# Eight graph-attention aggregations as seven half-products each, with the differences, sums and scores that this needs

## The chip, the cores and the metric

The kernel runs on one core of a Trainium2 chip, as one program of 31606 instructions. The metric is the device time of one execution in microseconds (us), the median over several runs. A core has a matrix engine (TensorE, "PE" in the profile, with its weight loads as "PEld"), a vector engine (VectorE, "DVE"), a scalar engine (ScalarE, "ACT"), a general engine (GpSimd, "POOL"), and a queue for transfers (SyncE, "SP"). Each engine runs its own instructions in order and waits for the others by semaphores. Matmuls write to PSUM, a memory of eight banks; the other data live in SBUF. All is fp32 here, and an fp32 matmul shows as two records in the trace.

## The reference, cut to what matters

A network of four layers over 512 nodes with 768 features. Only the graph part of layer 0 changes, a graph attention (GAT) of eight heads followed by one of a single head:

```python
def gat_layer(x, W, a_s, a_d, b, edge_index, concat):
    n = x.shape[0]
    H, C = a_s.shape
    h = (x @ W).reshape(n, H, C)
    src, dst = (edge_index[0], edge_index[1])
    alpha_s = jnp.einsum('nhc,hc->nh', h, a_s)
    alpha_d = jnp.einsum('nhc,hc->nh', h, a_d)
    e = jax.nn.leaky_relu(alpha_s[src] + alpha_d[dst], NEG_SLOPE)
    m = jax.ops.segment_max(e, dst, num_segments=n)
    e = jnp.exp(e - m[dst])
    denom = jax.ops.segment_sum(e, dst, num_segments=n)
    alpha = e / (denom[dst] + EPS)
    msg = h[src] * alpha[:, :, None]
    out = jax.ops.segment_sum(msg, dst, num_segments=n)
    ...
h = gat_layer(x, W1, a_src1, a_dst1, b1, edge_list, concat=True)
h = jax.nn.elu(h)
out = gat_layer(h, W2, a_src2, a_dst2, b2, edge_list, concat=True)
```

W1 is 768 x 6144 (eight heads of 768), W2 is 6144 x 768. With 16384 edges over 512 nodes the kernel works on a dense 512 x 512 matrix: `cnt` holds how often each edge occurs, and the softmax over a node's edges becomes a row of weights, so that a head's aggregation is a plain product of weights and features.

## The kernel before

Token-major tensors are four tiles of 128 nodes; feature-major ones six tiles of 128 features. A block product is made by seven half-products in place of eight (Strassen's scheme in Winograd's form): `SplitA` makes four sums of the left operand's quarters (L410 to L413 chunk by chunk, L420 to L423 whole), `SplitB` three differences of the right one's and one in place (L438 to L441, always on POOL), and `strassen` runs the seven products chunk by chunk (matmuls at L512) and combines them with one ACT copy (L527) and five DVE additions that read PSUM (L551, L554, L555, L560, L564). `strassen_token` gives token-major results, `strassen_feature` feature-major ones, and `strassen_add` (L605) adds its results into a tensor that exists.

One head i of layer 0 goes through these steps.

- `heads(i)` multiplies the normed nodes by W1's block i with seven half-products (the copy of h out of PSUM is at L823) and then takes two scores per node from h, source and target (`node_scores`, L796: four DVE instructions over 128x768 each, which read h and a row of coefficients, both in SBUF).
- `edge_weights` turns the scores into weights (`weighing`): four transposes spread the source scores (`row_of`, L329), four max-reductions with a penalty for missing edges follow (L743, which reads PSUM and the bf16 tile `off`), then the target score is added on ACT (L753), a leaky relu on DVE (L754), exp on ACT (L755), counts and row sums on DVE (L756), and the division (L763). `off` is made once, at the end of `edge_counts`, by four ACT instructions.
- `turned` transposes the weights on PE (L787) and copies them to `edge_wT` (L205 on ACT, L207 on DVE).
- `aggregate` multiplies features and weights plainly: six feature tiles times four node tiles, 24 matmuls with 512 columns (L901), each feature tile followed by `elu` (L802 to L804 on ACT, L805 on DVE) into gT and, for every second tile, by gT's sums on POOL (L410 to L413).
- `project` multiplies gT by W2's block and adds the result into h2 with `strassen_add` (DVE additions at L918).

The order across heads is a pipeline. In pass i of the main loop, the transposes of head i−1 are interleaved with the products of head i (the list `background`, one step at each product, by `tick`; `delayed(n)` lets n products go first). Then comes the aggregation of head i−1, then the edge weights of head i, then the projection of head i−1. `pinned` keeps what it wraps behind the last instruction of each engine before it; other instructions may be reordered by a scheduler. The tile of weights (`edge_w`) has one buffer, the weight matrices two, and their differences (`tw`) two.

Before head 0, `edge_counts` builds `cnt` from one-hot products of the edges (a comparison per 128 edges on DVE or ACT, L705 among them; sums on POOL, L722 and L723); 40 of its steps run ahead of head 0, the others beside it. The weights of head 1 are loaded, and their differences taken on POOL, when pass 1 begins.

Of the kernel before, what the change touches and what calls it, by code (L numbers as in the profile page):

```python
# [18 lines left out]
P = 128  # L19
# [78 lines left out]
def kernel(ctx: ExitStack, tc: tile.TileContext, a: dict, out: bass.AP):  # L98
# [296 lines left out]
    class SplitA:  # L395


        def __init__(self, xT, eng, ready=True):
            h = KC // 2
            self.st = big_tile("sx")[:, : 4 * h * HT].rearrange("p (i k n) -> p i k n", i=4, k=h)  # L400
            self.eng = eng
            self.a11, self.a12 = xT[:, :h, :HT], xT[:, h:, :HT]
            self.a21, self.a22 = xT[:, :h, HT:], xT[:, h:, HT:]
            self.s = [None] + [self.st[:, i] for i in range(4)]
            if ready:
                self.all_sums()
# [18 lines left out]
    def ready(src):  # L425

        return SplitB(split_weights(src))

    class SplitB:


        def __init__(self, w):
            h = KC // 2
            tt = diff_tile("tw").rearrange("p (i k n) -> p i k n", i=3, k=h)
            b11, b12 = w[:, :h, :HC], w[:, :h, HC:]
            b21, b22 = w[:, h:, :HC], w[:, h:, HC:]
            for k in range(h):
                G.tensor_sub(tt[:, 0, k], b22[:, k], b12[:, k])  # L438
                G.tensor_sub(b12[:, k], b12[:, k], b11[:, k])  # L439
                G.tensor_sub(tt[:, 1, k], b22[:, k], b12[:, k])  # L440
                G.tensor_sub(tt[:, 2, k], b21[:, k], tt[:, 1, k])  # L441
            self.b11, self.b21, self.b22 = b11, b21, b22
            self.t = [None, b12, tt[:, 1], tt[:, 0], tt[:, 2]]

    background = []

# [51 lines left out]
    def strassen(A, B, use, feature, then=None, extra=None, fresh=False):  # L498
# [5 lines left out]

        def product(bank, a, b, c, start, stop):
            tick()
            for k in range(KC // 2):
                if feature:
                    l, r = b[:, k, ts(c, P)], a[:, k, :]
                else:  # L510
                    l, r = a[:, k, ts(c, P)], b[:, k, :]
                T.matmul(bank, l, r, start=start and k == 0, stop=stop and k == KC // 2 - 1,  # L512
                         skip_group_check=True)

        def done(c, i, j, bank):
# [143 lines left out]
    counts = tc.tile_pool(name="counts", bufs=1, side="right")  # L659
    gone = counts.__enter__()  # L660
    cnt = gone.tile([P, NT, N], FP, name="cnt")
    off = gone.tile([P, NT, N], BF, name="off")
    cnt_dram = tc.dram_tile([P, NT, N], FP, name="cnt_dram")

    def reloaded(pool):
# [4 lines left out]
    def edge_counts(gp):  # L670
# [24 lines left out]
        for g in range(n_groups):  # L695
            js = range(EC * g // n_groups, EC * (g + 1) // n_groups)
            acc = [psum() for _ in range(2)]
            for j in js:
                oh = hots[j % len(hots)]
                if (j % 2 if j < 40 else j % 3 == 2):  # L700
                    S.activation(oh[:, :N], nodes, AF.Abs, bias=neg[:, j : j + 1])
                    S.activation(oh[:, :N], oh[:, :N], AF.Relu, bias=1.0, scale=-1.0)
                else:
                    V.tensor_scalar(oh[:, :N], nodes, ef[:, 0, j : j + 1], None, op0=ALU.is_equal)
                V.tensor_scalar(oh[:, N:], near if j < 32 else nodes[:, :HT], ef[:, 1, j : j + 1], far[:, j : j + 1],  # L705
                                op0=ALU.is_equal, op1=ALU.mult)
                for u in range(2):
                    T.matmul(acc[u], oh[:, N + u * P : N + (u + 1) * P], oh[:, :N],
                             start=j == js[0], stop=j == js[-1])
                yield  # L710
            for u in range(2):
                low, high = cnt[:, u, :], cnt[:, 2 + u, :]
                t = gp.tile([P, N], FP, name="up_t", bufs=2)
                S.activation(t, acc[u], AF.Identity, bias=part, scale=1.0 / HI)
                if g == 0:
                    V.tensor_scalar(high, t, MAGIC, -MAGIC, op0=ALU.add, op1=ALU.add)
                    V.scalar_tensor_tensor(low, high, -HI, acc[u], op0=ALU.mult, op1=ALU.add)
                else:
                    V.tensor_scalar(t, t, MAGIC, -MAGIC, op0=ALU.add, op1=ALU.add)
                    r = gp.tile([P, N], FP, name="up_r", bufs=1)  # L720
                    V.scalar_tensor_tensor(r, t, -HI, acc[u], op0=ALU.mult, op1=ALU.add)
                    G.tensor_add(high, high, t)  # L722
                    G.tensor_add(low, low, r)  # L723
        for t in range(NT):
            S.activation(off[:, t, :], cnt[:, t, :], AF.Relu, bias=bigc, scale=-BIG)
        nc.sync.dma_start(cnt_dram, cnt)

    def several(steps, n):
# [5 lines left out]
            yield  # L734


    def weighing(w, src4, dst4, cnt, off):

        srow = row_of(src4)
        yield  # L740
        mx = tiny(NT, name="ga_mx")
        for t in range(NT):
            V.tensor_tensor_reduce(w[:, t, :], srow, off[:, t, :], 1.0, -3.0e38,  # L743
                                   ALU.subtract, ALU.max, mx[:, t : t + 1])
        V.tensor_add(mx, mx, dst4)
        nm = tiny(NT, name="ga_nm")
# [18 lines left out]
    def weight_tile(gp):  # L765
        return gp.tile([P, NT, N], FP, tag="edge_w", name="edge_w", bufs=1)

    def edge_weights(src4, dst4, gp, cnt, off):
        w = weight_tile(gp)
        for _ in weighing(w, src4, dst4, cnt, off):  # L770
            pass
        return w

# [30 lines left out]
        S.activation(dst, dst, AF.Exp, scale=-1.0)  # L804
        V.scalar_tensor_tensor(dst, dst, -1.0, ps, op0=ALU.add, op1=ALU.max)  # L805

    def last_gat(h, as_row, ad_row, gp, cnt, off, between=None):

        s4, d4 = node_scores(h, row(as_row), gp), node_scores(h, row(ad_row), gp)
        ew = edge_weights(s4, d4, gp, cnt, off)  # L810
        made = between() if between else None
        wT = by_source(ew, gp)
        token_product(by_chunk(wT), lambda s: h[:, s, :], add_to_x)
        return made


    open_products()

    def heads(i):
        w1 = split_weights(a["L0_gnn_W1"][:, i * D : (i + 1) * D])  # L820
        B = pinned(lambda: SplitB(w1)) if i == 1 else SplitB(w1)
        h = token_major("h")
        strassen_token(xs, B, lambda t, c, ps: S.copy(h[:, t, ts(c, HC)], ps), None,  # L823
                       None if i else n0.rest)
        flush()
        return h, node_scores(h, row(f"g0_as{i}"), gp), node_scores(h, row(f"g0_ad{i}"), gp)

    with tc.tile_pool(name="graph", bufs=1) as gp:
        counting = edge_counts(gp)
        for _ in range(24):  # L830
            next(counting)
        n0 = Norm(x, "xn", 1e-5)
        for t in (0, 2, 1, 3):
            n0.chunk(t)
            if t == 1:
                n0.first()
        xs = n0.split
        raw_xn = tc.dram_tile([P, NT, D], FP, name="raw_xn")
        nc.sync.dma_start(raw_xn, n0.n)
        for _ in range(16):  # L840
            next(counting)
        background.append(several(counting, 7))
        loose.append(background[0])
        head0 = heads(0)
        drain()

    qkv = a["L0_mix_qkv_w"]
# [44 lines left out]
    with tc.tile_pool(name="gat0", bufs=2) as gp:  # L892
        h2 = token_major("h2")

        def aggregate(i, h, wT, norm=None):
            gT = feature_major("gT")
            sums = SplitA(gT, G, False)
            for n, f in enumerate((0, 3, 1, 4, 2, 5)):
                ps = psum()
                for s in range(NT):  # L900
                    T.matmul(ps, h[:, s, ts(f, P)], wT[:, s, :], start=s == 0, stop=s == NT - 1)  # L901
                elu(gT[:, f, :], ps, col("g0_b1", i * KC + f))
                if norm and n < NT:
                    norm.chunk(n)
                if f >= KC // 2:
                    sums.sums(f - KC // 2)
            return sums

        def project(i, sums):
# [29 lines left out]
        for i in range(9):  # L939
            if done:  # L940
                g, hg, ew = done
                wT = gp.tile([P, NT, N], FP, tag="edge_wT", name="edge_wT", bufs=wt_bufs[0])
                if i < 8:
                    if i == 1:
                        background.append(delayed(5, weighing(ew, s4, d4, cnt, off)))
                    background.append(delayed(0 if i == 1 else 8, turned(ew, wT)))
                else:
                    for _ in turned(ew, wT):
                        pass
            if i < 8:  # L950
                h, s4, d4 = heads(i) if i else head0
                drain()
            if done:
                norm = performer_norm() if i == 8 else None
                sums = aggregate(g, hg, wT, norm)
            if i < 8:
                done = i, h, edge_weights(s4, d4, gp, cnt, off) if i else weight_tile(gp)
            else:
                ys, va = performer_values(norm)
            if i:  # L960
                project(g, sums)
            if i == 2:
                degrees()
        x = load_x()
        qT = last_gat(h2, "g0_as", "g0_ad", gp, cnt, off, lambda: performer_features(ys, 0))
        add_row_to(x, row("g0_b2"))
    counts.__exit__(None, None, None)

# [1084 lines left out]
```

## Time and profile before

| quantity | value |
|---|---|
| median of 3 runs | 3097.74 us (3096.92 to 3099.75) |
| profiled execution, its own time | 3099.04 us |
| its span in the trace | 3097.2 us |
| mean granted TensorE clock | 0.992 of full speed |
| first to last of five equal periods of a head (from 235.35 us to 628.97 us) | 78.73 us each |
| PE busy in such a period | 77.6 us |
| DVE, ACT, POOL busy in such a period | 39.2, 22.1, 34.7 us |

A row of the profile's groups reads: line, engine, operation, output and inputs, shape and count, then the busy time in us and the mean of one in ns, and then the time that the engine idled just before such instructions, with what ended it. In the chain of waits every piece is the instruction that the next one had to wait for. In lists of instructions the first number is the start and the second the length in us. A busy time of PE includes the modelled end of each matmul, which overlaps the next one, so that lengths of records add up to more than the time that passes; the distance between their starts does not.

### The profile page before, as it was taken

Reading aid. Unit: us, or ns where it says so; the run is one execution under the profiler, and the core shown is the slowest. Engines: PE = TensorE matmul, PEld = TensorE weight load, DVE = VectorE, ACT = ScalarE, POOL = GpSimd, SP = SyncE. Lnnn points to the kernel's source line nnn. Section 1 sums busy time; section 2 is a strip of 40 time slices with the busy share of each in tenths; the row PEclk is TensorE's granted clock in tenths of the full one; section 3 lists DMA queues with packets and bytes.
Section 4 is the critical chain, followed back from the end, with each engine's and each line's share of the span. In section 5 each row is a group of like instructions: output and inputs, shape, how many; then the busy total and the mean of one; then the engine's idle time right before and its main releaser. Section 6 shows DMA issues by size and latency. Waiting matters only on the chain.

```text
span 3097.2 us, 31606 instructions
## 1 busy us (share of the span) xinstructions
PE 3005.4 (97%) x11757; PEld 2006.2 (65%) x11757; DVE 1482.7 (48%) x3416; ACT 749.7 (24%) x1434; POOL 1436.3 (46%) x1532
## 2 busy tenths in 40 slices
PE   7899999999999999999899999999999999999989
PEld 3455555556766777765675367877777776677755
DVE  9854444556256235446766435333333335462341
ACT  7322222252252112004432213100000012221111
POOL 3544444442516663655651444455544557355610
PEclk9999999999999999999999999999999999999999
DMA  3112212223202222321111512122221223122222
GB/s 116 56 70 72 72 72 72 71 92 82 82 1 97 92 92 93 118 92 57 61 72 62 148 67 97 67 92 92 92 90 68 88 92 123 60 89 77 99 80 62
DMA packets 92691, 253.63 MB, mean 82 GB/s; under 512 B 9889, under 2 KB 14881, under 8 KB 91514
## 3 DMA queue, kind: packets, MB, share of 16 engines
q1 hardware_dynamic: 92538, 251.61, 23.5%
q8 instruction: 93, 1.52, 0.2%
q14 instruction: 60, 0.49, 0.1%
HBM read 244.23 MB, written 7.36 MB: 81 GB/s over the span
## 4 chain that ended last, share of the span: by engine, by line
PE 86%; DVE 8%; POOL 2%; ACT 2%; issue 1%; DMA 0%; SPq 0%; POOLq 0%; ACTq 0%
PE ps L512 43%; PE ps L605 23%; PE ps L901 5%; PE ps L308 4%; PE ps L1109 1%; PE ps L1096 1%; PE ps L298 1%; PE ps L274 1%; PE ps L1934 1%; PE ps L1597 1%; POOL room L1455 1%; DVE edge_w L754 1%; DVE edge_w L743 1%; PE ps L1947 1%; PE ps L1324 1%
## 5 line engine op out<-in xcount | busy, mean ns | idle before, releaser
L438 POOL TENSOR_TENSOR tw<-w 128x384 f32<-128x384 f32 x246 | 247.8, 1017 | 953.4 <-DMA w<-in_L_gnn_W 308.1
L512 PE MATMUL ps<-sx,w 128*128 128x256 f32 x1188 | 316.9, 380 | 3.0 <-DVE sx L420 2.6
L512 PE MATMUL ps<-sx,tw 128*128 128x256 f32 x1188 | 290.3, 380 | 0.4
L605 PE MATMUL ps<-w,sx 128*128 128x384 f32 x720 | 256.4, 487 | 4.2 <-DVE sx L420 3.0
L440 POOL TENSOR_TENSOR tw<-w 128x384 f32<-128x384 f32 x246 | 254.0, 1039 | 9.6
L439 POOL TENSOR_TENSOR w<-w 128x384 f32<-128x384 f32 x246 | 252.7, 1036 | 8.8
L441 POOL TENSOR_TENSOR tw<-w,tw 128x384 f32<-128x384 f32 x246 | 251.7, 1030 | 10.3
L605 PE MATMUL ps<-tw,sx 128*128 128x384 f32 x720 | 250.5, 487 | 0.2 <-DVE x L654 0.2
L512 PEld LDWEIGHTS ps<-sx,w 128*128 128x128 f32 x1188 | 225.0, 190 | 38.2 <-PE ps L512 2.2
L512 PEld LDWEIGHTS ps<-sx,tw 128*128 128x128 f32 x1188 | 219.5, 190 | 43.0 <-DVE st_u L551 7.2
L527 ACT COPY st_p<-ps 128x256 f32<-128x256 f32 (+1 forms) x127 | 49.9, 394 | 722.1 <-PE ps L512 683.4
L551 DVE TENSOR_TENSOR st_u<-st_p,ps 128x256 f32<-128x256 f32 (+1 forms) x127 | 57.1, 450 | 346.7 <-PE ps L512 346.6
L605 PEld LDWEIGHTS ps<-tw,sx 128*128 128x128 f32 x720 | 136.0, 190 | 95.3 <-DVE x L1818 1.2
L605 PEld LDWEIGHTS ps<-w,sx 128*128 128x128 f32 x720 | 136.4, 190 | 94.3 <-POOL tw L441 4.1
L654 DVE TENSOR_TENSOR x<-x,ps 128x384 f32<-128x384 f32 x216 | 115.2, 552 | 164.1 <-PE ps L605 162.8
L512 PE MATMUL ps<-w,sx 128*128 128x384 f32 x456 | 170.3, 494 | 11.9 <-POOL w L439 10.1
L512 PE MATMUL ps<-xfT,w 128*128 128x256 f32 x720 | 176.8, 380 | 0.2
L512 PE MATMUL ps<-tw,sx 128*128 128x384 f32 x456 | 162.1, 491 | 4.9 <-DVE st_u L551 4.4
L901 PE MATMUL ps<-edge_wT,h 128*128 128x512 f32 x384 | 166.1, 592 | 0.0
L554 DVE TENSOR_TENSOR st_u<-st_p,ps 128x256 f32<-128x256 f32 (+1 forms) x127 | 57.1, 449 | 200.8 <-PE ps L512 200.8
L512 PEld LDWEIGHTS ps<-xfT,w 128*128 128x128 f32 x720 | 135.9, 190 | 24.1 <-issue 1.3
L605 PE MATMUL ps<-w,hid 128*128 128x384 f32 x432 | 142.9, 488 | 0.0
(484 smaller groups left out, 5063.6 us busy)
## 6 DMA issues: line engine op xcount, KB each, us to landing
w<-in_L_gnn_W SPq DMA_DIRECT2D x60, 768.0 KB, 6.8
w<-in_L_mix_fc_w SPq DMA_DIRECT2D x48, 768.0 KB, 6.3
row<-in_rows SPq DMA_DIRECT2D x39, 384.0 KB, 4.6
w<-in_L_mix_qkv_w SPq DMA_DIRECT2D x18, 768.0 KB, 5.2
w<-in_L_ffn_w SPq DMA_DIRECT2D x18, 768.0 KB, 7.0
w<-in_L_ffn_routed_gate SPq DMA_DIRECT2D x18, 768.0 KB, 5.9
w<-in_L_ffn_routed_up SPq DMA_DIRECT2D x18, 768.0 KB, 6.7
w<-in_L_ffn_routed_down SPq DMA_DIRECT2D x18, 768.0 KB, 5.7
```

What stands on the lines that cost most here:

```text
L308: T.matmul(ps, parts[k][:, ts(t, P)], w_of(k)[:, ts(c, HC)], start=k == 0, stop=k == n - 1)
L438: G.tensor_sub(tt[:, 0, k], b22[:, k], b12[:, k])
L439: G.tensor_sub(b12[:, k], b12[:, k], b11[:, k])
L440: G.tensor_sub(tt[:, 1, k], b22[:, k], b12[:, k])
L441: G.tensor_sub(tt[:, 2, k], b21[:, k], tt[:, 1, k])
L512: T.matmul(bank, l, r, start=start and k == 0, stop=stop and k == KC // 2 - 1, skip_group_check=True)
L527: S.copy(b["p1"], b["x"])
L551: V.tensor_add(b["u2"], b["p1r"], b["y"])
L554: V.tensor_add(u3, b["p1r"], b["y"])
L605: T.matmul(b[name], l[:, k, ts(m, P)], r[:, k, :], start=start and k == 0, stop=k == KC // 2 - 1, skip_group_check=True)
L654: V.tensor_add(x[:, t, ts(j, HC)], x[:, t, ts(j, HC)], ps)
L901: T.matmul(ps, h[:, s, ts(f, P)], wT[:, s, :], start=s == 0, stop=s == NT - 1)
```

## The change

The aggregation becomes a `strassen_feature` product: 42 matmuls with 256 columns per head, three chunks, with one ACT copy and five DVE additions per chunk. `elu` runs on twelve quarters of 128x256. Its operands need splitting, which a new generator `splitting` does in the place of `turned`: first `SplitB` of h on POOL (eight subtractions 128x384 in a pass, two of them in place in h), ordered behind the last POOL instruction of the aggregation before; then the transposes; then `SplitA` of the turned weights on DVE (four instructions over 128x512), into a tile that shares the single buffer of `edge_w`. It starts two products into the next head, not eight.

The target scores move out of `heads` to behind the aggregation, ahead of the edge weights (except for head 0). `off` goes; each weighing makes the penalty anew with four ACT instructions into the weight tile, and the max-reduction reads it there. W1 of heads 0 and 1 is loaded and split before head 0. In the counting, a copy of the node numbers in PSUM serves steps up to 40, not 32. `degrees` is pinned.

```diff
     class SplitA:
-        def __init__(self, xT, eng, ready=True):
-            h = KC // 2
-            self.st = big_tile("sx")[:, : 4 * h * HT].rearrange("p (i k n) -> p i k n", i=4, k=h)
+        def __init__(self, xT, eng, ready=True, st=None):
+            h = self.h = xT.shape[1] // 2
+            if st is None:
+                st = big_tile("sx")[:, : 4 * h * HT]
+            self.st = st.rearrange("p (i k n) -> p i k n", i=4, k=h)
...
     class SplitB:
-        def __init__(self, w):
-            h = KC // 2
-            tt = diff_tile("tw").rearrange("p (i k n) -> p i k n", i=3, k=h)
+        def __init__(self, w, tt=None):
+            h = w.shape[1] // 2
+            if tt is None:
+                tt = diff_tile("tw").rearrange("p (i k n) -> p i k n", i=3, k=h)
+                tt = [tt[:, i] for i in range(3)]
...
             for k in range(h):
-                G.tensor_sub(tt[:, 0, k], b22[:, k], b12[:, k])
+                G.tensor_sub(tt[0][:, k], b22[:, k], b12[:, k])
                 G.tensor_sub(b12[:, k], b12[:, k], b11[:, k])
...
-                V.tensor_scalar(oh[:, N:], near if j < 32 else nodes[:, :HT], ef[:, 1, j : j + 1], far[:, j : j + 1],
+                V.tensor_scalar(oh[:, N:], near if j < 40 else nodes[:, :HT], ef[:, 1, j : j + 1], far[:, j : j + 1],
...
-        for t in range(NT):
-            S.activation(off[:, t, :], cnt[:, t, :], AF.Relu, bias=bigc, scale=-BIG)
...
-    def weighing(w, src4, dst4, cnt, off):
+    def weighing(w, src4, dst4, cnt):
 
         srow = row_of(src4)
+        for t in range(NT):
+            S.activation(w[:, t, :], cnt[:, t, :], AF.Relu, bias=bigc, scale=-BIG)
         yield
         mx = tiny(NT, name="ga_mx")
         for t in range(NT):
-            V.tensor_tensor_reduce(w[:, t, :], srow, off[:, t, :], 1.0, -3.0e38,
+            V.tensor_tensor_reduce(w[:, t, :], srow, w[:, t, :], 1.0, -3.0e38,
...
+    def head_weights(i):
+        return ready(a["L0_gnn_W1"][:, i * D : (i + 1) * D])
+
     def heads(i):
-        w1 = split_weights(a["L0_gnn_W1"][:, i * D : (i + 1) * D])
-        B = pinned(lambda: SplitB(w1)) if i == 1 else SplitB(w1)
+        B = first_two.pop(0) if first_two else head_weights(i)
...
-        return h, node_scores(h, row(f"g0_as{i}"), gp), node_scores(h, row(f"g0_ad{i}"), gp)
+        return h, node_scores(h, row(f"g0_as{i}"), gp)
+
+    def target_scores(i, h):
+        return node_scores(h, row(f"g0_ad{i}"), gp)
...
+        first_two = [head_weights(i) for i in range(2)]
         for _ in range(16):
             next(counting)
...
+        def splitting(w, wT, h, both):
+
+            tt = gp.tile([P, 2, NT // 2, HC], FP, tag="h_diff", name="h_diff", bufs=1)
+            at = len(nc.cur_bb.bb.instructions)
+            both.append(SplitB(h, [Chunks([part_tile("p1r", HC) for _ in range(2)]), tt[:, 0], tt[:, 1]]))
+            if last_sums:
+                for ins in nc.cur_bb.bb.instructions[at:]:
+                    if ins.engine == mybir.EngineType.Pool:
+                        tc.add_manual_dep(ins, last_sums[-1], mybir.DependencyInfo(
+                            mybir.DependencyClass.NoSync, mybir.DependencyReason.DATA), reason="pinned")
+            yield
+            yield from turned(w, wT)
+            both.append(SplitA(wT, V, True, weight_tile(gp).rearrange("p t n -> p (t n)")))
+
-        def aggregate(i, h, wT, norm=None):
+        def aggregate(i, hB, wA, norm=None):
             gT = feature_major("gT")
             sums = SplitA(gT, G, False)
-            for n, f in enumerate((0, 3, 1, 4, 2, 5)):
-                ps = psum()
-                for s in range(NT):
-                    T.matmul(ps, h[:, s, ts(f, P)], wT[:, s, :], start=s == 0, stop=s == NT - 1)
-                elu(gT[:, f, :], ps, col("g0_b1", i * KC + f))
-                if norm and n < NT:
-                    norm.chunk(n)
-                if f >= KC // 2:
-                    sums.sums(f - KC // 2)
+
+            def use(c, n, j, ps):
+                f = 3 * j + c
+                elu(gT[:, f, ts(n, HT)], ps, col("g0_b1", i * KC + f))
+
+            def then(c):
+                sums.sums(c)
...
+            strassen_feature(wA, hB, use, then)
+            flush()
+            last_sums.append(next(ins.name for ins in reversed(nc.cur_bb.bb.instructions)
+                                  if ins.engine == mybir.EngineType.Pool))
             return sums
...
                 if i < 8:
                     if i == 1:
-                        background.append(delayed(5, weighing(ew, s4, d4, cnt, off)))
-                    background.append(delayed(0 if i == 1 else 8, turned(ew, wT)))
+                        background.append(delayed(5, weighing(ew, s4, d4, cnt)))
+                both = []
+                parts = splitting(ew, wT, hg, both)
+                if i < 8:
+                    background.append(delayed(2, parts) if i > 1 else parts)
...
             if done:
                 norm = performer_norm() if i == 8 else None
-                sums = aggregate(g, hg, wT, norm)
+                sums = aggregate(g, *both, norm)
+            if 0 < i < 8:
+                d4 = pinned(lambda: target_scores(i, h))
...
             if i == 2:
-                degrees()
+                pinned(degrees)
```

## The prediction

> **What bounds the kernel now.** I read the page's engine shares, the waits of PE, the chain of waits around one head, and the instructions of DVE and POOL there.
>
> ```profile
> PE 3005.4 (97%) x11757; PEld 2006.2 (65%) x11757; DVE 1482.7 (48%) x3416; ACT 749.7 (24%) x1434; POOL 1436.3 (46%) x1532
> PE 86%; DVE 8%; POOL 2%; ACT 2%; issue 1%; DMA 0%; SPq 0%; POOLq 0%; ACTq 0%
> L901 PE MATMUL ps<-edge_wT,h 128*128 128x512 f32 x384 | 166.1, 592 | 0.0
> ```
>
> TensorE bounds the program, so fewer matmul cycles are worth having wherever PE still finds work. But 97% is no distance to a limit; what counts is what PE waits for:
>
> ```profile
> PE ps L512 <- POOL w L439: 10.1, 2, 6.7
> PE ps L605 <- DVE h L918: 5.5, 5, 1.1
> ```
>
> The first wait is head 1's weights at the start; the second comes once in each of heads 2 to 6. Cutting the trace at the first matmul of each head gives five periods of 78.73 us. One end of an aggregation (E = 492.1), as the chain of waits has it:
>
> ```profile
> 485.68 6.44 PE ps L901 x15
> 492.12 0.45 PE ps L329 x4
> ...
> 492.60 0.69 DVE edge_w L743
> ...
> 498.22 1.73 DVE edge_w L754 x2
> 499.95 2.45 DVE edge_w L756 x8
> 502.40 0.47 DVE h L918
> ...
> 503.98 1.24 PE ps L605 x3
> ```
>
> The reader should see that the next head's edge weights (L743, L754, L756) fill DVE from E+0.5 to E+10.3, and the adds of `project` (L918) stand behind them in DVE's queue. PE finds work for 10.8 us, then stands 1.1 us for the third add. So the boundary is already DVE-bound by a hair: what DVE gets more there, PE waits.
>
> **The seven half-products.** A product of 128x512 is two records; the 48 records of one aggregation take 20.60 us back to back, 0.429 each. Of 128x256, 210 records elsewhere run in 45.60 us, 0.217. Per head: 48 x 0.429 = 20.6 becomes 42 x 2 x 0.217 = 18.2, −2.4 us; eight heads −19.5. The page's mean durations (592 ns, 380 ns) would say 28.4 to 31.9, a loss. The Trainium skill (Perfetto Trace Analysis, Identifying the Most-Contended Engine) warns that busy time of pipelined matmuls is a bad metric; the pitch above is what this trace shows, and I take it.
>
> The additions in the aggregation (per chunk an ACT copy 0.37, five DVE adds 0.43; twelve elu quarters at 0.47 + 0.38 + 0.42 on ACT instead of six at 0.66 + 0.60 + 0.63) come to 16.4 us of ACT in 18.2 us of PE: hidden inside, but the last quarter of gT comes at about E+4.2 instead of E+3.6. SplitA of wT (4 x 0.61 on DVE) lies in the next head's products, where DVE is under half busy: nothing, and 2.4 us if DVE were full. The four Relus per head take ACT 2.5 us just after the last elu, beside DVE's scores: nothing.
>
> **Target scores behind the aggregation.** In the heads' own time this saves little: the last copies of h end about 1.3 us after the products instead of 2.1, and ACT's in the aggregation start a trifle late, +0.13. At the boundary it puts 4 x 0.88 us on DVE, alternating with the four max-reductions (0.61), from E+4.2. Then L754 with its small steps 3.8, L756 4 x 0.61 = 2.5, and the adds, of which the last that matters ends about 1 us later: 4.2 + 6.0 + 3.8 + 2.5 + 1 = E+17.5, against E+11.9. PE's cover until then, in the new order: row_of 0.55, six matmuls of 128x384 on gT itself 3.87 (0.645 each, two records of 0.323), twelve on its sums 7.74, six of the next head 3.87, together 16.0 us. Stall 1.5, alone hardly worse than today.
>
> **Features' differences behind the last sums.** Eight POOL subtractions 128x384 per head follow the last sums of gT. They land beside DVE's edge weights, which have two SBUF inputs. The rows:
>
> ```profile
> 116.53 0.98 DVE L796 SCALAR_TENSOR_TENSOR st_u<-h,row 128x768 bf16<-128x768 f32 x1
> ...
> 117.44 1.74 DVE L796 SCALAR_TENSOR_TENSOR st_u<-h,row 128x768 bf16<-128x768 f32 x1
> ...
> 495.81 1.18 POOL L410 TENSOR_TENSOR sx<-gT 128x256 f32<-128x256 f32 x1 [0.71 <-DVE ga_mx L745]
> ...
> 498.13 1.82 DVE L754 SCALAR_TENSOR_TENSOR edge_w<-edge_w 128x512 f32<-128x512 f32 x2
> ```
>
> The same score takes 0.98 alone and 1.74 beside POOL's differences of W; L754 has a pitch of 0.60 alone and 0.87 beside POOL's sums, whose 0.73 becomes 1.18. L743, with an input in PSUM, keeps 0.61 throughout. The Trainium skill (SBUF — State Buffer, Who interferes with whom) names it: a DVE instruction with two SBUF inputs contends with a GpSimd instruction that reads SBUF, over a port pair that one holds for a whole instruction. By that rule each subtraction met costs DVE its whole 0.8 us; all eight would cost 6.4 and the last four sums 0.5 more. By the columns of the diff alone (POOL is 46% busy) the cost is nothing. This rule speaks against the change. Some of the eight fall in DVE's waits for ACT or beside PSUM reads; I take a bit over half, 4.4 x 0.8 = 3.5, + 0.5: the third add ends at E+21.5, PE waits 5.5. Ends: 0 and 6.9.
>
> The queues these steps are moved past hold nothing that is late: POOL stands idle for 25.3 us after the last sums until W's transfer lands (524.69), so 6.4 us more go before W's differences for nothing. On SP the targets' row is reloaded only when the scores of the head before release it, at about E+10; the six loads of W queued behind it went out from 519.16 on, E+27, so 17 us remain.
>
> **Per steady head**: −2.4 + 0.13 + (5.5 − 1.64 of today's small stalls) = +1.6. Behind aggregations 1, 3, 4 and 5 the new order has those six matmuls of the next head; behind 0 only four (cover 1.3 less), behind 2 only two (2.6 less). Sum over aggregations 0 to 5: 6 x 1.6 + 3.9 = **+13.5**.
>
> **Aggregations 6 and 7.** Behind 6 no head follows, so no fillers; today `project` 6 runs with 0.75 us of waits, and its adds will stand behind head 7's edge weights: 5 to 10 us of stall less 2.4, I take **+6** (ends +2, +9). Aggregation 7: −2.4, + 0.65 for sums of wT behind the 16 transposes with nothing beside them, + 2.5 for the performer's norm waiting behind more elu pieces: **+0.7**.
>
> **The start.** W1 of head 1 is loaded and differenced on POOL before head 0, into POOL's idle time from 25.6 to 48.4 us; its load is moved past one load of two rows on SP alone (1.46 us, rows used 100 us later). That takes away 10.1 us of the first wait above and 0.65 behind it. What is late next: head 1's third half-product waits for a DVE add behind eight scores of head 0 that still run beside POOL's count additions and head 0's differences (1.67 each): 3 us; head 0's weights come later by 0.5; sums of wT stand in front of aggregation 0 behind scores: 2.4; a reading of node numbers from PSUM for eight more columns (0.46 for 0.26): with POOL's new work in the counting about 1. Net −10.7 + 6.9 = **−4** (ends −9, 0).
>
> **Dropped `off`**: four Relus once less, a tile of SBUF less; nothing on the path.
>
> Sum: 13.5 + 6 + 0.7 − 4 = +16 us on the execution of 3099.04 (span 3097.2), which lies 1.3 above the median of 3097.74 and within the runs' spread. From the median: **3113 us**.
>
> **Rivals.** A difference below 0.2%, 6.2 us, can't be told from no change.
>
> A. *Boundary contended* (above): 3105 to 3121. Chance 0.41.
>
> B. *The port is mostly free.* If the differences slip into DVE's waits, the add ends at E+17.5 and a head costs −2.4; over six −14 + 3.9; the start −7, project 6 +2, aggregation 7 nothing: −15, **3083**. For it: POOL's eight can begin only when the target scores have read h, and DVE waits for ACT between L743 and L754; against: L754 and L756 follow at once and both have two SBUF inputs. It decides as soon as fewer than two of eight meet. Chance 0.24.
>
> C. *Half and half.* Add at E+19.5: a head −0.4, six +1.5; +4 +0.7 −5: **3099**, no change. Chance 0.2.
>
> D. *All eight meet.* Stall 8.4 per head, +4.5 each and 3.9: +31; project 6 +8, aggregation 7 +1.5, start −3: **3135**. For it: POOL blocks DVE for whole instructions, as 1.74 twice in a row shows; against: DVE's small steps leave gaps. Chance 0.15.
>
> That the halves don't shorten PE at all (waits between a chunk's products for the DVE adds that free a bank) is a further way to D: no row shows 128x256 chunks of only two matmuls a product. Ends: 0 and 2.4 us per head; I take 0, as the 128x256 chunks of three (L512) wait 3.4 us in 2376 records.
>
> **Range.** From B's 3083, less 1, to just short of D's: 3082 to 3133; beside it the likeliest's own 3105 to 3121. Faster 0.24, within 0.2% 0.20, slower 0.56.
>
> **What would show it.** Right: in a head's period about 80.3 us; PE's wait for the add of `project` 5 to 6 us once a head; the scores and L754's successor at over 1 us beside POOL's h_diff; aggregation 18.2 us without gaps; no wait of head 1 for W1. Wrong: periods below 77 with scores at 0.88 (B); an aggregation of over 19 us with gaps; a wait in the heads' products for the sums of wT.

## The result and the profile after

The changed kernel takes 3131.71 us (median of 4 runs, 3128.92 to 3136.02) against 3098.74 us before, a ratio of 1.0107 (95% interval 1.0092 to 1.0121). The profiled execution has a span of 3130.8 us, 33.6 more than before. The sign was forecast; the size was not: 15 us, less than half of it. The engine shares, the chain of waits and PE's waits that answer to the lines of before:

```profile
PE 3006.5 (96%) x12045; PEld 2061.5 (66%) x12045; DVE 1596.6 (51%) x3616; ACT 790.9 (25%) x1632; POOL 1534.6 (49%) x1596
PE 81%; DVE 12%; ACT 4%; POOL 2%; issue 1%; DMA 0%; SPq 0%; POOLq 0%; ACTq 0%; DVEq 0%
```

```profile
PE ps L618 <- DVE h L960: 18.9, 6, 8.6
...
PE ps L525 <- DVE st_u L564: 11.1, 10, 5.6
PE ps L618 <- POOL sx L412: 6.0, 7, 1.8
PE ps L618 <- POOL sx L413: 5.4, 7, 0.8
```

The columns of the second are the total in us, how often, and the longest. The wait for the adds of `project` (L918 before, L960 now) has gone from 5.5 to 18.9 us, POOL's sums of gT are a new wait of 11.4, and the wait for W1 is replaced by one of 5.6 for an addition (L564).

Both traces cut at the first matmul of each aggregation give the place of the 33.6 us. A half-speed window is a stretch in which the clock record of TensorE grants 0.5.

| stretch | before | after | change | predicted | half speed, before / after |
|---|---|---|---|---|---|
| start to aggregation 0 | 156.30 | 152.27 | −4.0 | −4 | 17.1 / 10.2 |
| period 0 | 78.88 | 90.82 | +11.9 | +2.9 | 0 / 10.2 |
| period 1 | 78.73 | 81.69 | +3.0 | +1.6 | 0 / 3.4 |
| period 2 | 78.72 | 81.24 | +2.5 | +4.2 | 0 / 0 |
| period 3 | 78.72 | 80.20 | +1.5 | +1.6 | 0 / 0 |
| period 4 | 78.72 | 81.68 | +3.0 | +1.6 | 0 / 3.4 |
| period 5 | 78.73 | 81.67 | +2.9 | +1.6 | 0 / 3.4 |
| period 6 | 50.89 | 60.90 | +10.0 | +6 | 0 / 10.2 |
| aggregation 7 | 20.60 | 20.15 | −0.5 | +0.7 | 0 / 0 |
| all behind it | 2396.90 | 2400.17 | +3.3 | 0 | 31.8 / 38.6 |

One steady head of the changed kernel, DVE, then POOL, then the waits of PE, with E = 424.34 as the end of the aggregation (start, length):

```profile
427.95 0.95 DVE L808 SCALAR_TENSOR_TENSOR st_u<-h,row 128x768 bf16<-128x768 f32 x1
...
435.72 0.95 DVE L759 SCALAR_TENSOR_TENSOR ga_nm<-ga_mx 128x4 f32<-128x4 f32 x1
...
440.10 1.48 DVE L768 SCALAR_TENSOR_TENSOR edge_w<-edge_w,cnt 128x512 f32<-128x512 f32 x1
...
441.50 1.47 DVE L768 SCALAR_TENSOR_TENSOR edge_w<-edge_w,cnt 128x512 f32<-128x512 f32 x1
...
444.31 0.54 DVE L960 TENSOR_TENSOR h<-h,ps 128x384 f32<-128x384 f32 x1
```

```profile
432.43 1.53 POOL L413 TENSOR_TENSOR sx<-sx,gT 128x256 f32<-128x256 f32 x1
...
439.70 1.33 POOL L453 TENSOR_TENSOR h_diff<-h 128x384 f32<-128x384 f32 x1
440.99 1.44 POOL L452 TENSOR_TENSOR h<-h 128x384 f32<-128x384 f32 x1
442.39 1.44 POOL L454 TENSOR_TENSOR h_diff<-h,h_diff 128x384 f32<-128x384 f32 x1
```

```profile
431.03 0.91 PE L618 MATMUL ps<-w,sx 128*128 128x384 f32 x2 [0.92 <-POOL sx L412]
...
434.01 0.91 PE L618 MATMUL ps<-tw,sx 128*128 128x384 f32 x2 [0.78 <-POOL sx L413]
...
444.90 1.56 PE L618 MATMUL ps<-w,gT 128*128 128x384 f32 x4 [2.05 <-DVE h L960]
```

The reader should see the two engines in step: one L768 at a pitch of 1.40 per subtraction at 1.44, where alone they take 0.61 and 1.0. The scores (L808) keep their pitch of 0.88; a max-reduction that reads PSUM stands between any two of them. There it is POOL that pays: its sums go from 0.73 to 1.53, and PE waits 0.92 + 0.78 us for them. The add that PE needs is done at E+20.5.

### The profile page after: what moved, and what is told of

It reads as the page before. It is cut to its first block, busy times and chain, and to the rows that moved or that the text cites. A ratio compares the mean times of both kernels' runs of the same rounds, so it can differ in the third digit from the quotient of the medians.

```text
span 3130.8 us, 32710 instructions
## 1 busy us (share of the span) xinstructions
PE 3006.5 (96%) x12045; PEld 2061.5 (66%) x12045; DVE 1596.6 (51%) x3616; ACT 790.9 (25%) x1632; POOL 1534.6 (49%) x1596
## 4 chain that ended last, share of the span: by engine, by line
PE 81%; DVE 12%; ACT 4%; POOL 2%; issue 1%; DMA 0%; SPq 0%; POOLq 0%; ACTq 0%; DVEq 0%
PE ps L525 44%; PE ps L618 23%; PE ps L308 4%; DVE st_u L808 1%; DVE edge_w L768 1%; DVE oh L717 1%; PE ps L1159 1%; PE ps L1146 1%; PE ps L298 1%; ACT ps L814 1%; PE ps L274 1%; PE ps L1984 1%; PE ps L1647 1%; ACT gT L816 1%; POOL room L1505 1%
## 5 line engine op out<-in xcount | busy, mean ns | idle before, releaser
L564 DVE TENSOR_TENSOR st_u<-st_p,ps 128x256 f32<-128x256 f32 (+1 forms) x151 | 67.2, 445 | 288.9 <-PE ps L525 288.7
L618 PEld LDWEIGHTS ps<-tw,sx 128*128 128x128 f32 x720 | 135.5, 190 | 103.4 <-POOL sx L413 9.8
L540 ACT COPY st_p<-ps 128x256 f32<-128x256 f32 (+1 forms) x151 | 59.0, 391 | 562.7 <-PE ps L525 523.0
L567 DVE TENSOR_TENSOR st_u<-st_p,ps 128x256 f32<-128x256 f32 (+1 forms) x151 | 67.2, 445 | 220.2 <-PE ps L525 220.1
L525 PEld LDWEIGHTS ps<-tw,sx 128*128 128x128 f32 x456 | 86.2, 193 | 71.3 <-DVE st_u L564 16.5
```

What stands on the lines that cost most here:

```text
L540: S.copy(b["p1"], b["x"])
L564: V.tensor_add(b["u2"], b["p1r"], b["y"])
L567: V.tensor_add(u3, b["p1r"], b["y"])
L618: T.matmul(b[name], l[:, k, ts(m, P)], r[:, k, :], start=start and k == 0, stop=k == KC // 2 - 1, skip_group_check=True)
```

## The experiments

All times are medians beside the kernel before on the same chip (3098.7 to 3099.3); periods come from one profile each.

**Undoing one part at a time.** *start_only* is the kernel before with the early W1, and with the node numbers in PSUM up to step 40:

```diff
+        first_two = [head_weights(i) for i in range(2)]
...
-                V.tensor_scalar(oh[:, N:], near if j < 32 else nodes[:, :HT], ...
+                V.tensor_scalar(oh[:, N:], near if j < 40 else nodes[:, :HT], ...
...
+        B = first_two.pop(0) if first_two else head_weights(i)
```

> The kernel before with head 1's W1 loaded and differenced early and PSUM node numbers up to step 40; nothing else. If the prediction's account of the start holds (10.1 + 0.65 us of waits go, about 1 comes back in the counting), aggregation 0 starts about 9 to 10 us earlier than before (156.3 to about 147) and the program takes about 3089. If what replaced the wait in the changed kernel (5.6 us for an addition behind the scores) comes from the early differences themselves and not from the scores and the features' differences beside them, it starts only about 4 us earlier: 3094.

It took 3093.44 us, ratio 0.9982 (0.9975 to 0.9989). Aggregation 0 starts at 150.39, 5.9 us earlier. The waits for W1 are gone, and PE now waits 5.30 us for an addition that stands in DVE's queue behind the reduction for the degrees (2.29) and head 0's eight scores, of which only the last two run beside POOL (1.74 instead of 0.95). So the replacement wait comes up as soon as W1 is early; it needs neither differences of h nor moved scores.

*no_h_diff* leaves the subtractions on h out (the half-products take plain quarters of h, and the output is another):

```diff
...
-            both.append(SplitB(h, [Chunks([part_tile("p1r", HC) for _ in range(2)]), tt[:, 0], tt[:, 1]]))
...
+            both.append(Same(b11, b21, b22, [None, b12, b22, b21, b11]))
```

> The changed kernel without the eight subtractions of SplitB on h (the seven half-products take plain quarters of h, so the aggregation's output is another). Theory 'port': these subtractions are what stretches L768 from a pitch of 0.61 to 1.40; without them L768 is back at 0.61, the third add of project comes about 3.2 us earlier, PE's wait of 2.05 per head is gone, periods 1 to 5 fall from 81.3 to about 79, or 78 where the half-speed clock windows go too, project 6's wait falls from 8.6 to about 5.5: about 3112. Theory 'scores': the four target scores alone keep DVE late; L768 changes but the wait of PE stays above 1.5 and the time within 5 us of 3132.

3096.40 us, ratio 0.9992 (0.9984 to 1.0001): 35 us less than the changed kernel, against 20 expected. Of these, 17.0 came in periods 1 to 5 and 7.2 in period 6; 6.5 in the start and 5.2 in period 0 were not in the expectation. Periods 1 to 5 are 77.65 (78.90 in the second), period 6 is 53.70, the start 145.75, period 0 85.62, and there is no half-speed window in periods 1 to 6. DVE's row for the same instructions (L768 is L773 here, L759 is L764):

```profile
417.61 0.15 DVE L764 SCALAR_TENSOR_TENSOR ga_nm<-ga_mx 128x4 f32<-128x4 f32 x1
...
420.64 0.68 DVE L773 SCALAR_TENSOR_TENSOR edge_w<-edge_w,cnt 128x512 f32<-128x512 f32 x1
...
421.86 0.55 DVE L960 TENSOR_TENSOR h<-h,ps 128x384 f32<-128x384 f32 x1
```

Even the instruction over four columns takes 0.15 instead of 0.95. The add ends at E+16.2 (E = 406.24), and PE no longer waits for it. Without the eight subtractions per head nothing is lost, so they account for all of the loss; nothing is gained either, which the later runs take up.

*scores_back* returns the target scores to the end of each head's products:

```diff
...
-        return h, node_scores(h, row(f"g0_as{i}"), gp)
+        return h, node_scores(h, row(f"g0_as{i}"), gp), target_scores(i, h)
...
```

> The changed kernel with the target scores back at the end of each head's products. Theory 'scores' (3.5 us of DVE go from behind the aggregation, and POOL's last sums are no longer held): both waits of PE per head, 1.7 for POOL's sums and 2.05 for the add, are gone; periods about 77, project 6's wait about 5, together about 3105. Theory 'port': the features' differences now start earlier and meet L766 and L768 both, eight of them at 0.8 us, so the add is hardly earlier, PE's wait stays at 1.5 to 2 and only the 1.7 for the sums goes: about 3120.

3148.34 us, ratio 1.0158 (1.0144 to 1.0172): worse than the changed kernel, which neither theory had. PE around one head:

```profile
434.51 4.04 PE L618 MATMUL ps<-w,gT 128*128 128x384 f32 x12
438.38 2.10 PE L618 MATMUL ps<-w,sx 128*128 128x384 f32 x6
...
444.19 2.10 PE L618 MATMUL ps<-tw,sx 128*128 128x384 f32 x6
451.52 3.83 PE L618 MATMUL ps<-w,gT 128*128 128x384 f32 x6 [5.24 <-DVE h L959]
```

The wait for POOL's sums is gone, as expected, and the add comes at E+17.4 instead of E+20.5. But the scheduler now puts no matmul of the next head here: PE's cover is 12.2 us and its wait 5.24. A wait of 1.30 at the start of each aggregation (its first addition behind eight scores) and 9.02 in aggregation 0 come on top. What covers a wait is part of the change as much as the wait.

*both_back* also moves the differences of h to DVE, in the next head's products:

> The changed kernel with the target scores back in the heads and the features' differences on DVE, two groups of four in the next head's products, so that neither lies at the end of an aggregation. If scores and port together are the cause, the third add ends at about E+13 as against PE's cover of 16: no wait there, periods 76.0 to 76.6 (the 78.7 of before less 2.4), no half-speed windows in the heads, about 3085 to 3092, below the kernel before. If the cost is in the half-products themselves (copies, additions, elu quarters), periods stay above 79 and the time above 3110.

3111.30 us, ratio 1.0041 (1.0029 to 1.0054). The wait for the add is gone in the steady heads and periods 2 to 5 are 78.7, 78.1, 77.3 and 78.1; but DVE's subtractions stand in front of additions that PE needs (0.6 to 3.4 us), and aggregation 0 waits 11.45 us for a copy of `edge_wT` on DVE: period 0 takes 95.4, with 20.5 us at half speed. So neither theory fits: the periods are below 79 and the time is above 3110. The moved work was hidden from one queue and exposed in another.

*plain_agg* is the changed kernel with the plain aggregation of before (early W1, moved target scores and four Relus stay):

```diff
...
-            strassen_feature(wA, hB, use, then)
...
+            for n, f in enumerate((0, 3, 1, 4, 2, 5)):
+                ps = psum()
+                for s in range(NT):
+                    T.matmul(ps, h[:, s, ts(f, P)], wT[:, s, :], start=s == 0, stop=s == NT - 1)
+                elu(gT[:, f, :], ps, col("g0_b1", i * KC + f))
...
```

> The changed kernel with the plain aggregation of before (24 matmuls with 512 columns, six elu tiles) and therefore without differences of h and sums of wT; the early W1, the moved target scores and the four Relus stay. It gives the worth of the half-products: if they save PE 2.4 us per head as predicted, periods are about 2.3 above those without differences, 79.5 to 80; period 0 has no wait for wT's sums, about 80 against 85.6; together 3100 to 3105. If the half-products save less (periods within 1 of 77.65), about 3090.

3090.28 us, ratio 0.9972 (0.9960 to 0.9983): faster than both. Periods 2 to 5 are 78.63, only 1.0 above those without differences. The seven half-products shorten the aggregation by nearly what was predicted (first to last matmul 18.1 instead of 20.2), but PE then waits 1.7 us for POOL's sums, where the plain form waits 0.84 for an add. The time is that of the expectation's second case, for another reason: the saving is there, and waits take half of it.

**Moving the subtractions in time.** *h_later* leaves all work in, and lets a one-column copy on POOL wait for the last edge weight before the subtractions:

```diff
+            if last_sums:
+                G.tensor_copy(tiny(1, name="gate"), w[:, NT - 1, 0:1])
+                yield
             tt = gp.tile([P, 2, NT // 2, HC], FP, tag="h_diff", name="h_diff", bufs=1)
```

> The changed kernel with one thing moved: on POOL the features' differences of heads 1 to 7 stand behind a one-column copy that waits for the last edge weight of the same head, so they run after DVE's edge weights, in POOL's idle time before W2 lands. Nothing is left out. Theory 'port': L768 back to a pitch of 0.61, no wait for the third add, periods 1 to 5 as without the differences (77.65, with 78.9 in the second), project 6 about 54; start and period 0 nearly as in the changed kernel (head 0's differences stay where they are): about 3131.7 - 4 x 5 - 7 = 3105. Theory 'too much work for POOL or for the products' (not the place but the differences themselves): POOL is late for W2 or for the aggregation, new waits appear there, and the time stays above 3120.

POOL in one steady head (E = 412.34):

```profile
422.03 1.15 POOL L415 TENSOR_TENSOR sx<-gT,sx 128x256 f32<-128x256 f32 x1
431.23 0.19 POOL L919 COPY gate<-edge_w 128x1 f32<-128x1 f32 x1 [8.06 <-DVE edge_w L775]
431.37 1.96 POOL L451 TENSOR_TENSOR st_p1r<-h 128x384 f32<-128x384 f32 x2
```

3110.46 us, ratio 1.0038 (1.0025 to 1.0050), 5 us above the 3105 expected. The same instructions on the same engine, from E+19.0 instead of E+10.8, are worth 21 us: L768 is back at a pitch of 0.61, periods 1 to 5 are 78.8 to 79.3, no half-speed window in any, and period 0 falls from 90.8 to 84.0. Period 6 stays at 59.5, with its wait of 8.62, since the last pass runs unpinned and its subtractions slipped ahead of the copy. (With the copy the transposes also begin one product later, which no run separates.) The 1.2 us above *no_h_diff* are a wait for L564 behind the sums of `edge_wT`, which now meet W2's differences.

*plain0_later* adds a plain aggregation for head 0:

> As h_later, and head 0 alone aggregated plainly, so that no differences of h run beside head 0's scores in the start and no sums of wT stand before aggregation 0. Theory 'port and queue order': the start is as without differences (145.8 instead of 152.3), period 0 about 80 instead of 90.8, the rest as in h_later: 3131.7 - 6.5 - 11 - 20 - 7 = about 3088. If period 0's loss came from the additions of project 0 behind head 1's edge weights rather than from aggregation 0, period 0 stays above 84: 3093.

3101.89 us, ratio 1.0008 (1.0001 to 1.0014). Start 145.61 and period 0 79.06, both as expected; period 6 is still 60.0. The total is 14 us above the 3088 expected, mainly because periods 1 to 5 gave 11.7 us where 20 had been taken, and period 6 0.9 where 7 had. Period 0's +11.9, then, splits into 6.8 for head 1's subtractions (*h_later*) and 5.0 for splitting head 0's aggregation, whose waits in the changed kernel are:

```profile
157.10 1.22 PE L525 MATMUL ps<-edge_wT,h 128*128 128x256 f32 x2 [2.48 <-DVE edge_wT L207]
159.38 2.04 PE L525 MATMUL ps<-edge_w,h 128*128 128x256 f32 x4 [1.06 <-DVE edge_w L422]
...
201.00 3.90 PE L618 MATMUL ps<-w,gT 128*128 128x384 f32 x6 [2.92 <-DVE h L207]
```

The second row is four records in 2.04 us where others take 1.03, the third six in 3.90 where others take 2.20: PE works at half speed there.

*plain0_later_p6* also emits project 6 ahead of head 7's edge weights:

```diff
+            if i == 7:
+                project(g, sums)
             if i < 8:
                 done = i, h, edge_weights(s4, d4, gp, cnt) if i else weight_tile(gp)
...
-            if i:
+            if i and i != 7:
                 project(g, sums)
```

> As plain0_later, and project 6 emitted ahead of head 7's edge weights, whose adds DVE then takes first. Nothing is queued on PE behind project 6 but the transposes of head 7's weights. Theory 'adds behind edge weights': the 4 us that PE waits in period 6 without differences go, period 6 is about 50 to 51 instead of 53.7, 3085. Rival: the edge weights, now behind, come late for the transposes and period 6 stays at 53 to 55: no gain.

3109.77 us, ratio 1.0035 (1.0022 to 1.0049). The wait for the adds goes and the transposes wait 16.29 us for the last edge weight: period 6 is 68.9. The rival held, by more than it said.

*plain0_later_8* instead pins the steps of the last pass, so that head 7's subtractions wait, too:

> As plain0_later, and in the last pass, too, the differences of head 7 are held behind the copy that waits for the last edge weight (there they had been free to run ahead of it, and period 6 kept its wait of 8.62 us). Theory 'port': period 6 falls from 60.0 to about 53.7, as without differences, or 52; the time from 3101.9 to about 3095. Rival: period 6's wait comes from having no products of a next head behind project 6, whatever POOL does: it stays at 8 us and the time at 3102.

3099.30 us, ratio 0.9998 (0.9990 to 1.0006). Period 6 falls from 60.0 to 55.5 and its wait from 8.62 to 3.19, the same as in *no_h_diff*: most of it was the port.

*later_scores_back* then returns the target scores of heads 2 to 7 to the heads:

> As plain0_later_8, and the target scores of heads 2 to 7 back at the end of the heads' products. With the differences out of the way the scores no longer push them into the edge weights. Theory: the 1.7 us that PE waits for POOL's last sums (held by the scores) go, 1.3 us come at the start of the aggregation (its first addition behind eight scores on DVE), periods 77.9 to 78.4 against 78.8; about 3091, near the plain aggregation's 3090. Rival: as in scores_back the scores' place costs more than it gives, periods above 79 and the time above 3096.

3080.55 us, ratio 0.9942 (0.9928 to 0.9955): faster than the kernel before by 18 us, than the plain aggregation by 10 and than *start_only*, which has the early W1 and the scores in the heads as well, by 13: more than either theory gave. Periods are 76.6 to 77.6 and period 6 is 49.9. POOL and PE in one head (E = 474.60):

```profile
481.80 0.75 POOL L413 TENSOR_TENSOR sx<-sx,gT 128x256 f32<-128x256 f32 x1
482.62 1.06 POOL L415 TENSOR_TENSOR sx<-gT,sx 128x256 f32<-128x256 f32 x1
491.74 0.18 POOL L920 COPY gate<-edge_w 128x1 f32<-128x1 f32 x1 [8.06 <-DVE edge_w L775]
491.88 1.97 POOL L451 TENSOR_TENSOR st_p1r<-h 128x384 f32<-128x384 f32 x2
...
508.03 1.00 POOL L451 TENSOR_TENSOR tw<-w 128x384 f32<-128x384 f32 x1 [8.46 <-DMA w<-in_L_gnn_W]
```

```profile
483.90 2.10 PE L618 MATMUL ps<-w,sx 128*128 128x384 f32 x6
486.17 2.20 PE L618 MATMUL ps<-w,gT 128*128 128x384 f32 x6 [0.17 <-DVE h L975]
```

The reader should see that POOL waits 8 us on purpose, does the subtractions in pairs at 1.0 each, and still waits 8.46 us for W2 afterwards. Nearly the same move of the scores (here without head 1's) that cost 17 us beside the subtractions gains 19 once they are away. The add now ends at E+11.5 instead of E+17.4, so that PE needs no matmuls of the next head to cover it.

**The clock.** *after_2* and *after_3* are the changed kernel again, for a second and third profile:

> The changed kernel once more, for a second profile. Theory 'clock': the half-speed windows that follow PE's waits of 2.05 us fall by the phase of the clock's own sampling, so they appear in other heads than in the first profile (there in periods 1, 4 and 5, not in 2 and 3), and a period is 81.7 where one falls and 80.2 where none does, with the same waits. Rival: 80.2 in period 3 belongs to that head (its order of instructions), and the same periods come out again whatever the clock.

> As after_2, a third profile: the same two theories. In all three profiles together, each period with a half-speed window of 3.4 us should be 1.3 to 1.7 us longer than the same period without one, and the tail behind aggregation 7, whose code is unchanged, should be longer by half of what its half-speed windows exceed those of the kernel before.

One run each, 3132.76 and 3129.61 us. Periods 2, 3 and 4 of the first profile and of the second (columns: window, its length, busy time of PE, PEld, DVE, ACT, POOL with instruction counts, the granted clock, DMA share, GB/s):

```profile
324.78:406.02 81.24, 76.27 (x273) 49.12 (x272) 53.59 (x107) 28.27 (x64) 47.92 (x44) 1.00 0.20 68
406.02:486.22 80.20, 76.17 (x273) 49.16 (x272) 53.13 (x107) 27.61 (x63) 48.04 (x44) 1.00 0.19 69
486.22:567.90 81.68, 77.66 (x274) 49.98 (x272) 53.41 (x107) 27.61 (x63) 47.99 (x44) 0.98 0.19 68
```

```profile
326.10:409.03 82.93, 77.96 (x273) 50.05 (x272) 53.54 (x107) 28.26 (x64) 47.93 (x44) 0.98 0.19 67
409.03:489.22 80.19, 76.16 (x273) 49.26 (x272) 52.76 (x107) 27.59 (x63) 48.15 (x44) 1.00 0.20 70
489.22:570.87 81.65, 77.64 (x273) 50.09 (x272) 53.31 (x107) 27.58 (x63) 48.02 (x44) 0.98 0.19 68
```

Period 2 with the same waits is 81.24 at full clock and 82.93 with a window; periods 3 and 4 have the same waits and differ by 1.48. So a window costs 1.5 to 1.7 us. (Period 1 takes 81.69 and 82.77 with a window and 81.55 without, but its other waits differ by up to 1.1 us; with these taken off, the window comes to 1.2 and 1.5.) That the windows fall in other heads each time mostly failed: 4 and 5 have one in all three profiles, 3 in none; only 1 and 2 changed.

Yet the windows do not belong to the heads, as the traces show. Within one profile all windows start at whole multiples of 3.413 us from each other (in the first, those at 283.07, 525.41 and 607.33 lie 71 and 24 such steps apart), and each lasts a whole number of such steps, but for the one that the program's end cuts. Laid on these steps, nine of the fifteen waits of 2.05 us in periods 1 to 5 of the three profiles lie within one step (to 0.03 us), and the next step ran at half speed; six cross from one step into the next, with at most 1.64 us in either, and no window came. Period 3's wait crosses in all three profiles, those of periods 4 and 5 in none. Length alone does not decide: in *no_h_diff* the wait of 3.19 us in period 6 is split into 1.33 and 1.85, and it brought no window. Between 130 us and aggregation 7 in all fourteen traces, each of the 34 full-speed steps in which PE waited 2.01 us or more was followed by half speed, and none of the 2248 in which it waited 1.85 or less. In the rest of the program the border is less sharp, between 1.5 and 2.0 us.

The tail behind aggregation 7 was 2398.75 and 2399.70 us in the second and third profile, with 35.1 and 35.2 us at half speed.

## Why the prediction was right in sign and wrong in size

- **Half-products: right.** First to last matmul of an aggregation is 18.1 us in heads 1 and 3 to 6 (18.5 in head 2, with a short wait) instead of 20.2, as the pitch of 0.217 gave; the mean durations of the page would have forecast a loss. (By these pitches eight heads save 18.9 us, not the 19.5 that was written; that figure did not enter the sum.)
- **The port: right.** The subtractions meet the edge weights, the add ends at E+20.5 (predicted E+21.5) and without them at E+16.2 (E+17.5): 4.3 us between the two, where 4.0 was forecast. Weighing the skill's rule against the free POOL decided the sign. By the prediction's own pitches, with 2.2 us for the transposes, PE's work in one period is now about 74.7 us, so PE loses 5.5 in period 3 (80.20), which is the size forecast. But the forecast put all of it on the add. The trace lists 2.05 us for the add and 1.7 for POOL's sums, which the prediction had slowed on DVE's side only, and what PE loses at the sums comes off the wait for the add. So the steady +1.6 (+1.5 in period 3) is right in its sum and in part lucky in its terms. Periods 1 to 5 together: +12.8, predicted +10.6.
- **The step that failed: each wait of PE was priced at its own length.** "The third add ends at E+21.5, PE waits 5.5" has no term for the clock. In the kernel before there is no half-speed window from 133 us to the end of the graph part; in the changed one they follow the new waits: 3.4 us in periods 1, 4 and 5 (1.5 each, 4.5 together), 10.2 in period 0, where PE works through some 9 (4.4), and 10.2 in period 6, where it works through 5.8 (2.9). That is 11.8 of the 17.6 us that the sum was short. Start and tail nearly cancel in this: over the whole profile PE worked 65.5 us at half speed instead of 41.5, and half of the 24.0 more is 12.0. With *no_h_diff* and *h_later* the waits in periods 1 to 5 shrink or move, and the windows there are gone.
- **Period 0, "1.3 less cover": too small.** This is the second term that was mis-sized, by some 4.6 us beside the clock. Period 0 was priced like a steady head with two matmuls less. It has what no other head has: the sums of `edge_wT` stand directly before the aggregation (4.1 us of waits with the copy of p1; 2.4 were counted, in the start), and project 0 copies into h2 behind the edge weights (1.46 + 2.92).
- **Period 6: +6, with the end at +9, measured +10.** 8.62 us for the add, and the clock behind it.
- **The start: −4, right by luck.** The wait behind the scores was 5.6 and not 3; the 2.4 for the sums of `edge_wT` came after aggregation 0 had started, in period 0. PE's waits in the start fell by only 1.9 us (17.8 to 15.9). The rest is the clock, which the prediction did not have: PE worked 9.3 us at half speed there instead of 14.4, worth 2.6.
- **Aggregation 7: −0.5 for +0.7.** Its waits were 1.1 us in all, 0.6 of them for the sums. What the prediction put here for the performer's norm (2.5) shows in the tail, as a new wait of 1.35 for a copy of yT. That wait and 2.1 for 4.3 us more work at half speed make the tail's +3.3. The other two profiles fit: 1.4 and 3.3 us more work at half speed, the same wait, and tails of +1.9 and +2.8.

Rival D had the right total by the wrong way. Seven of the eight subtractions had started before the add was done, but they made it 4.3 us later and not 6.9, and the steady waits for sums and add were 3.75 and not 8.4; the clock and period 0 made up for that.

## What to carry to other kernels

Work put into an idle engine was free here only where nothing beside it shared its port; the two places of the same subtractions differ by 21 us. So read the durations of both engines where they overlap, and hold the moved work back, by a small copy that waits for the last of its rival, until the port is free. Price a new wait of PE with the clock that may follow it, here 1.5 to 1.7 us on top of a wait of 2 us in nine cases of fifteen, and with what covered it before. Test a part of a change together with its neighbours: nearly the same move of four scores per head lost 17 us in one company and gained 19 in the other.

## What the runs showed of the hardware that was not expected

- Beside POOL's subtractions a DVE instruction over 128x4 took 0.95 us instead of 0.15. Small as it is, it waits about as long as one POOL subtraction takes alone (1.0).
- The engine that loses depends on the neighbours. Scores that alternate with a reader of PSUM kept their pitch of 0.88 and POOL went from 0.73 to 1.53; consecutive L768 went from 0.61 to 1.40 and POOL's subtractions from 1.0 to 1.44.
- Waits of 2.05 us brought a half-speed window of 3.4 us in three, four and two of five equal periods of the three profiles, by their place on steps of 3.413 us: 2.01 us within one step were enough, 1.85 were not, and a wait of 3.19 split over two steps brought none. The Trainium skill (TensorE: Matmul & The Clock Gate, Why this matters for your kernels) warns of idle gaps above about 3 us; here the measurement decides, and shorter ones were enough.
